# Attention over 4096 positions: where k's tiles and v's rows lie in SBUF

## The chip, the cores and the metric

The kernel runs on one core of one Trainium2 chip. The metric is the device time in microseconds: the median of 3 runs. Before the change it is 2519.33 us (2519.18 to 2519.79). The profile is of one execution, with a span of 2516.5 us and a mean granted TensorE clock of 0.999 of full speed.

## The reference

For each of 4 images of 64 x 64 positions with 256 channels, three projections q, k (128 channels each) and v (256 channels) are formed, then attention without a scale, then a sum with the input:

```
q = x @ Wq + bq; k = x @ Wk + bk; v = x @ Wv + bv     # float32
pq = q.reshape(B, -1, N); pk = ...; pv = ...          # N = 64 * 64 = 4096, a plain reshape
energy = einsum('bcn,bcm->bnm', pq, pk)
attention = softmax(energy, axis=-1)
out = gamma * einsum('bcm,bnm->bcn', pv, attention) + x
```

All is float32, and the result has to be nearly so.

## The kernel before

**Two programs.** The function has a fast program (lines 199 to 529), which takes exponentials without subtracting a maximum, and a general one (line 531 on), which runs only if the sums of the exponentials leave a range. The fast one checks that range at its end: `guard` (line 412) compares all sums `zall` with two limits, puts the answers in the tile `ok`, and reduces them to one word, `again`. In the profiled execution only the fast program ran.

**Splitting.** TensorE multiplies in float32r. To get nearly float32 from it, each operand is split into forms: h (an upper part, a slightly scaled rounded copy), l (what h leaves) and d (a combination of both). `halved` does this for q and k, `project_v` for v (vh, vl, vd), `upper` and `halves` for the exponentials. Each product then takes three matrix products: h with h, l with l, d with d.

**Tiling.** Per image, NG = 16 groups g of NB = 256 columns of output, and for each group NU = 8 steps t of 4 blocks of 128 positions: `STEPS` = 128 per image, 512 in all. One step does:

- `energy` (line 298): 12 products of 256 columns. The stationary operand (weights) is a 128 x 128 slice of the tile `k`, the moving one a form of the tile `q` (two runs of 128 columns). Results go to `sa` and `sb` in PSUM, and ScalarE takes exponentials into `x` and `y` (line 315).
- `join` (x times y, VectorE), `upper` (h, ScalarE), `halves` (l and d, VectorE).
- `attend` (line 344), twice: 12 products each, four with h and `vh`, four with l and `vl`, four with d and `vd`. The weights are slices of h, l or d; the moving operand is row m of v's form, with m = 2t, 2t + 16, 2t + 1, 2t + 17 for the four. The rows of `vh` and `vl` have C + 2 = 258 columns: 256 of v, and two of ones, which give the sums of the exponentials. Rows of `vd` have 256.

**Order.** The order of every engine's instructions is written out by hand (`manual_schedule`): the loop at line 490 puts step u's attention after the energies of step u + 3 (`LOOK`), so that TensorE always has work that does not wait for the exponentials. `load_k` (line 292) fetches k's forms from DRAM, 768 KB a step, five steps ahead into 3 buffers.

**Addresses.** A tile pool's tiles lie one after the other in SBUF, in the order const, xpool, xtpool, qkv, ppool, work, kpool; each buffer's size is rounded up to 32 bytes per partition. `q` (3072 bytes, 2 buffers), `r` and `ra` are in `work`, the tile `k` (6144 bytes, 3 buffers) and `f` (3072 bytes, 2 buffers) in `kpool`, which comes last. `vh` and `vl` are in `qkv`, `ok` and `zall` in `const`. The pools fill SBUF up to 128 bytes: the last buffer of k ends at byte 229,248 of 229,376.

The last group of the last image is finished by `finish_last` (line 427), all others by `whole` and `finish`; both take the factors `r` (gamma over the sums) from `factors` (line 377).

Of the kernel before, what the change touches and what calls it, by code (L numbers as in the profile page):

```python
# [9 lines left out]
F32 = mybir.dt.float32  # L10
F32R = mybir.dt.float32r
I32 = mybir.dt.int32
AF = mybir.ActivationFunctionType
ALU = mybir.AluOpType
# [6 lines left out]
def kernel(  # L21
# [36 lines left out]
    nc = tc.nc  # L58
    B, W, H, C = x.shape
    P = 128  # L60
    N = W * H
    C2 = C // 2
    NM = N // P
# [14 lines left out]
    const = ctx.enter_context(tc.tile_pool(name="const", bufs=1))  # L78
# [8 lines left out]
    ones = const.tile([P, P], F32, name="ones")  # L87
# [12 lines left out]
    gam = const.tile([P, 1], F32, name="gam")  # L100
# [73 lines left out]
    NB = 256  # L174
    NJ = NB // P
    NG = N // NB
    NU = NM // 4
    STEPS = NG * NU
    LOOK = 3
    E = 2.0**-12  # L180


# [1 line left out]

    again = const.tile([P, 1], I32, name="again")
    zs = const.tile([P, 1], F32, name="zs")
    ok = const.tile([P, B * NG * NJ], F32, name="ok")

    zall = const.tile([P, B * NG, NJ], F32, name="zall")
    bv4_sb = const.tile([P, KC], F32, name="bv4_sb")  # L190
    nc.gpsimd.tensor_scalar(bv4_sb, bv_sb, 1.0 / E, None, ALU.mult)

# [6 lines left out]
    with ExitStack() as fast:  # L199
# [4 lines left out]
        xpool, xtpool, qkv = pool("xpool", 3), pool("xtpool", 3), pool("qkv", 1)  # L204
        ppool, work, kpool = pool("ppool", 2), pool("work", 2), pool("kpool", 3)
# [3 lines left out]
        ps_t = pool("ps_t", 1, space=PSUM)  # L209


        vh = qkv.tile([P, NM, C + 2], F32R, tag="vh", name="vh")
        vl = qkv.tile([P, NM, C + 2], F32R, tag="vl", name="vl")
        vd = qkv.tile([P, NM, C], F32R, tag="vd", name="vd")
        for t in (vh, vl):
            nc.scalar.copy(t[:, :, C:], ones[:, : 2 * NM].rearrange("p (m t) -> p m t", t=2))

        images, qd, kf, units, loads, now = [], {}, {}, {}, {}, {}

# [13 lines left out]
        def image(b):  # L233
# [7 lines left out]
            def v_out(i):  # L241
                now["v4"] = work.tile([P, KC, C], F32, tag="v4", name=f"v4_{b}_{i}")
                return now["v4"], bv4_sb, 1.0 / E

# [7 lines left out]
        def halved(f, x):  # L252

            h = f[:, :, 0, :]
            nc.scalar.activation(h, x, AF.Identity, scale=UPPER / 64)
            for j, s, op in ((1, -64.0, ALU.add), (2, 64.0 * (1.0 + E), ALU.subtract)):
                nc.vector.scalar_tensor_tensor(
# [12 lines left out]
        def project_v(b, i):  # L270
# [3 lines left out]
            h = vh[:, m, :C]  # L274
            nc.scalar.activation(h, v4, AF.Identity, scale=UPPER * E)

            for t, f in ((vl, 1.0 / E), (vd, 1.0 / E + 1.0)):
                nc.vector.scalar_tensor_tensor(
# [19 lines left out]
        def energy(b, u, k):  # L298
# [10 lines left out]
            for i in range(2):  # L309
                for to, f, first, last in ((sa, 0, True, False), (sa, 1, False, True), (sb, 2, True, True)):  # L310
                    nc.tensor.matmul(  # L311
                        to[:, i], kt[:, 2 * k + i, f, :], q[:, :, f, :], start=first, stop=last
                    )
            for to, sp, scale in ((x, sa, (1.0 + E) / E), (y, sb, -1.0 / E)):
                nc.scalar.activation(  # L315
# [28 lines left out]
        def attend(b, u, j):  # L344
            g, t = divmod(u, NU)
            if t == j == 0:
                now["acc"] = [
                    ps_o.tile([P, C + 2], F32, tag=f"a{j}", name=f"a{j}_{b}_{g}")
                    for j in range(NJ)
                ]  # L350
                now["bb"] = ps_o.tile([P, NJ, C], F32, tag="bb", name=f"bb_{b}_{g}")
            h, l, d = units[b, u]
            a, bb = now["acc"][j], now["bb"]
            n = slice(j * P, (j + 1) * P)
            for out_, left, right in ((a, h, vh), (a, l, vl), (bb[:, j, :], d, vd)):
                for i in range(4):
                    m = 2 * t + i // 2 + NI * (i % 2)

                    nc.tensor.matmul(  # L359
                        out_,  # L360
                        left[:, i, n],
                        right[:, m, :],
                        start=(t == i == 0 and (left is h or left is d and j == 0)),
                        stop=(t == NU - 1 and i == 3 and left is not h),
                        skip_group_check=True,
                    )
            if t == NU - 1 and j == NJ - 1 and (b, g) != (B - 1, NG - 1):
                now["o"] = work.tile([P, NJ, C], F32, tag="o", name=f"o_{b}_{g}")
                nc.scalar.copy(now["o"], bb)

        def sums(b, g):
            for j in range(NJ):
                a = now["acc"][j]
                nc.vector.tensor_copy(zall[:, b * NG + g, j : j + 1], a[:, C : C + 1])

        def factors(b, g):

            r = work.tile([P, NJ], F32, tag="r", name=f"r_{b}_{g}")
            nc.vector.reciprocal(r, zall[:, b * NG + g, :])
            nc.vector.tensor_tensor(r, r, gam.to_broadcast([P, NJ]), ALU.mult)  # L380
            return r

        def whole(b, g):

# [7 lines left out]

        def finish(b, g, o, xr):
            yield
            r = factors(b, g)
            for j in range(NJ):
                nc.scalar.activation(  # L397
                    o[:, j, :], o[:, j, :], AF.Identity, scale=r[:, j : j + 1]
                )
            yield  # L400
            yield
            tp = ps_t.tile([P, 2, NB], F32, tag="t", name=f"ot_{b}_{g}")
            for s in range(2):
                for j in range(NJ):
                    nc.tensor.transpose(
                        tp[:, s, j * P : (j + 1) * P], o[:, j, s * P : (s + 1) * P], ident
                    )
            yield
            nc.vector.tensor_tensor(xr, xr, tp, ALU.add)
            nc.gpsimd.dma_start(ov[b, g], xr)  # L410

        def guard():

            z = zall.rearrange("p n j -> p (n j)")
            nc.vector.tensor_scalar(ok, z, Z_LOW, None, ALU.is_ge)
            nc.vector.scalar_tensor_tensor(ok, z, Z_HIGH, ok, ALU.is_le, ALU.mult)
            yield
            nc.vector.tensor_reduce(zs, ok, AX.X, ALU.min)
            nc.vector.tensor_scalar(zs, zs, 0.5, None, ALU.is_lt)
            zp = ps_s.tile([P, 1], F32, tag="b", name="zp")  # L420
            nc.tensor.matmul(zp, ones, zs, start=True, stop=True)
            yield
            nc.vector.tensor_copy(again, zp)
            yield
            yield

        def finish_last(b, g, xr):

            sums(b, g)
            r = factors(b, g)  # L430
            check = guard()
            ra = work.tile([P, NJ], F32, tag="ra", name="ra", bufs=1)
            nc.vector.tensor_scalar(ra, r, 1.0 + E, None, ALU.mult)
            o = work.tile([P, NJ, C], F32, tag="o", name=f"o_{b}_{g}")
            tps = []
            for j in range(NJ):
                next(check)
                nc.scalar.activation(
                    o[:, j, :], now["bb"][:, j, :], AF.Identity, scale=r[:, j : j + 1]
                )  # L440
                nc.vector.scalar_tensor_tensor(
                    o[:, j, :], now["acc"][j][:, :C], ra[:, j : j + 1], o[:, j, :], ALU.mult, ALU.add
                )
                tp = (ps_t, ps_s)[j].tile([P, 2, P], F32, tag="ta"[j], name=f"ot_{b}_{g}_{j}")
                for s in range(2):
                    nc.tensor.transpose(tp[:, s, :], o[:, j, s * P : (s + 1) * P], ident)
                tps.append(tp)
            for j in range(NJ):
                next(check)
                n = slice(j * P, (j + 1) * P)  # L450
                nc.vector.tensor_tensor(xr[:, :, n], xr[:, :, n], tps[j], ALU.add)
            nc.sync.dma_start(ov[b, g], xr)
# [18 lines left out]
        for b in range(B):  # L471
# [18 lines left out]
            for u in range(STEPS):  # L490
                g, t = divmod(u, NU)
                ahead = u + LOOK
                if ahead // NU + 1 < NG and ahead % NU == 3:
# [23 lines left out]
                for j in range(NJ):  # L517
                    attend(b, u, j)
                if (b, u) == (B - 1, STEPS - 1):
                    finish_last(b, g, loads.pop((b, "x", g)))  # L520
                elif t == NU - 1:
                    whole(b, g)
                    start(finish(b, g, now["o"], loads.pop((b, "x", g))))
# [7 lines left out]
    NB = 512  # L531
    NG = N // NB
    NJ = NB // P
    NP = NM // 2
    xg, og = columns(x, NB), columns(out, NB)
    with tc.If(nc.values_load(again[0:1, 0:1]) > 0), ExitStack() as general:
# [3 lines left out]
        xpool, xtpool, qkv = pool("gx", 2), pool("gxt", 2), pool("gqkv", 1)  # L540
        ppool, work = pool("gp", NP + 2), pool("gw", 1)
# [3 lines left out]
        for b in range(B):  # L545
# [16 lines left out]
            for g in range(NG):  # L562
                ps = []
                mx = work.tile([P, 2, NB], F32, tag="mx", name=f"gmx_{b}_{g}")
                for t in range(NP):
# [9 lines left out]
                    p = ppool.tile([P, 2, NB], F32, tag="p", name=f"gp_{b}_{g}_{t}")  # L575
# [52 lines left out]
                r = work.tile([P, NB], F32, tag="r", name=f"gr_{b}_{g}")  # L628
                nc.vector.reciprocal(r, zb)
                for s in range(2):  # L630
                    y = work.tile([P, NB], F32, tag="y", name=f"gy_{b}_{g}_{s}")
# [33 lines left out]
```

## Time and profile before

| | value |
|---|---|
| time, median of 3 | 2519.33 us |
| span of the profiled execution | 2516.5 us |
| LDWEIGHTS in `attend`, h / l / d | 189 ns each, 4096 of each kind |
| LDWEIGHTS in `energy` | 188 ns, 6144 |
| VectorE, join / l / d | 1222 / 1218 / 1218 ns, 512 of each |
| ScalarE, exponentials of sa / sb | 595 / 599 ns, 1024 of each |
| k's load | 512 of 768 KB, 4.8 us from issue to landing |
| DMA | 198 GB/s in the mean |

PE is TensorE's matrix products, PEld its loads of weights, which overlap the products; DVE is VectorE, ACT is ScalarE, POOL is GpSimd. In a group's row the figures after the bar are busy time in us and mean duration in ns, and after a second bar the idle time of the engine just before these instructions and what ended it. Products are pipelined: one starts long before the one ahead of it is at its end, so TensorE's pace has to be read from starts.

### The profile page before, as it was taken

What the parts mean: (1) busy time and instruction counts of PE and PEld (TensorE: products, weight loads), DVE (VectorE), ACT (ScalarE), POOL (GpSimd) and SP (SyncE); (2) the same over time, 40 slices, a digit from 0 to 9 for tenths busy, and PEclk for the clock granted to TensorE, in tenths of its full rate; (3) what the DMA queues carried; (4) which work ended last, traced back from release to release, by engine and by line L of the source; (5) the groups of instructions that cost most, each with busy time, mean ns of one, the idle gap of its engine ahead of it and who ended that gap; (6) DMA issues with size and microseconds to landing.
All of it is one profiled execution on the core that took longest, in us unless ns stands there. A gap on an engine that the chain in (4) does not pass through costs nothing.

```text
span 2516.5 us, 50017 instructions
## 1 busy us (share of the span) xinstructions
PE 2497.4 (99%) x19982; PEld 2455.1 (98%) x19982; DVE 2102.5 (84%) x2440; ACT 1806.1 (72%) x3138; POOL 424.6 (17%) x780
## 2 busy tenths in 40 slices
PE   9999999999999999999999999999999999999998
PEld 8999999999899999999989999999998999999998
DVE  5888888888688888888868888888886888888887
ACT  5777777776677777777667777777766777777775
POOL 4211111111411111111041111111114111111110
PEclk9999999999999999999999999999999999999999
DMA  7666666664766666666476666666648666666663
GB/s 238 214 192 210 198 203 197 193 207 147 236 214 189 206 198 201 201 191 205 138 243 220 194 192 207 200 206 194 190 143 254 213 197 195 201 200 206 198 191 108
DMA packets 137407, 498.92 MB, mean 198 GB/s; under 512 B 15536, under 2 KB 57264, under 8 KB 137168
## 3 DMA queue, kind: packets, MB, share of 16 engines
q0 software_dynamic: 92320, 453.17, 57.4%
q1 hardware_dynamic: 44304, 42.22, 5.6%
q8 instruction: 160, 2.62, 0.4%
q14 instruction: 79, 0.65, 0.1%
q10 hardware_dynamic: 544, 0.26, 0.0%
HBM read 445.25 MB, written 50.33 MB: 197 GB/s over the span
## 4 chain that ended last, share of the span: by engine, by line


## 5 line engine op out<-in xcount | busy, mean ns | idle before, releaser
L315 ACT ACTIVATE x<-sa 128x512 f32<-128x512 f32 x1024 | 609.5, 595 | 429.6 <-PE sa L311 367.6
L325 DVE TENSOR_TENSOR x<-x,y 128x1024 f32<-128x1024 f32 x512 | 625.4, 1222 | 172.9 <-ACT y L315 172.9
L311 PE MATMUL sa<-q,k 128*128 128x256 f32 x4096 | 759.2, 282 | 6.3 <-ACT x L315 6.0
L359 PE MATMUL a<-vh,h 128*128 128x258 f32 x4096 | 662.4, 284 | 0.0
L359 PE MATMUL a<-vl,l 128*128 128x258 f32 x4096 | 660.3, 283 | 0.0
L359 PE MATMUL bb<-vd,d 128*128 128x256 f32 x4096 | 651.9, 281 | 0.0
L311 PEld LDWEIGHTS sa<-q,k 128*128 128x128 f32 x4096 | 627.1, 188 | 8.0 <-ACT x L315 6.9
L336 DVE TENSOR_TENSOR l<-x,h 128x1024 fp32r<-128x1024 f32 x512 | 623.6, 1218 | 0.0
L339 DVE SCALAR_TENSOR_TENSOR d<-h,x 128x1024 fp32r<-128x1024 f32 x512 | 623.5, 1218 | 0.0
L315 ACT ACTIVATE y<-sb 128x512 f32<-128x512 f32 x1024 | 613.1, 599 | 0.0
L311 PE MATMUL sb<-q,k 128*128 128x256 f32 x2048 | 580.4, 283 | 0.0
L330 ACT ACTIVATE h<-x 128x1024 fp32r<-128x1024 f32 x512 | 543.5, 1061 | 34.9 <-DVE x L325 34.0
L359 PEld LDWEIGHTS a<-vl,l 128*128 128x128 f32 x4096 | 563.8, 189 | 0.0
L359 PEld LDWEIGHTS a<-vh,h 128*128 128x128 f32 x4096 | 561.5, 189 | 0.0
L359 PEld LDWEIGHTS bb<-vd,d 128*128 128x128 f32 x4096 | 557.6, 189 | 0.0
L295 POOL DMA_DIRECT2D k<-kf x512 | 279.7, 546 | 1508.1 <-PE sb L311 1476.0
L311 PEld LDWEIGHTS sb<-q,k 128*128 128x128 f32 x2048 | 385.4, 188 | 8.7 <-ACT y L315 0.8
L136 PE MATMUL qk<-wqk_sb,xts 128*128 128x256 f32 x512 | 121.5, 380 | 0.0
L157 PE MATMUL v<-xts,wv_sb 128*128 128x256 f32 x512 | 120.3, 379 | 0.0
L157 PEld LDWEIGHTS v<-xts,wv_sb 128*128 128x128 f32 x512 | 97.3, 190 | 13.2
L397 ACT ACTIVATE o<-o,r 128x256 f32<-128x256 f32 x126 | 57.4, 502 | 72.4 <-DVE r L380 72.4
L136 PEld LDWEIGHTS qk<-wqk_sb,xts 128*128 128x128 f32 x512 | 92.7, 191 | 10.1
(54 smaller groups left out, 884.5 us busy)
## 6 DMA issues: line engine op xcount, KB each, us to landing
k<-kf POOLq DMA_DIRECT2D x512, 768.0 KB, 4.8
x<-in_x_dram SPq DMA_DIRECT2D x128, 256.0 KB, 3.6
kf<-f POOLq DMA_DIRECT2D x64, 384.0 KB, 4.2
out_dram<-x POOLq DMA_DIRECT2D x63, 256.0 KB, 2.5
qd<-qks POOLq DMA_DIRECT2D x128, 64.0 KB, 2.9
qr<-qd SPq DMA_DIRECT2D x64, 128.0 KB, 3.1
wv_sb<-in_L_conv_Wv_dram POOLq DMA_DIRECT2D x1, 256.0 KB, 5.4
out_dram<-x SPq DMA_DIRECT2D x1, 256.0 KB, 3.9
```

What stands on the lines that cost most here:

```text
L136: nc.tensor.matmul(qk[:, s, :], self.xt[i][:, k, s, :], wqk_sb[:, k, :], start=(k == 0), stop=(k == KC - 1),)
L157: nc.tensor.matmul(vp[:, eh, :], wv_sb[:, k, eh * P : (eh + 1) * P], self.xt[i][:, k].rearrange("p s a -> p (s a)"), start=(k == 0), stop= ...
L295: nc.gpsimd.dma_start(t.rearrange("p (i s) f d -> p i s (f d)", s=2), kf[b, u % NU])
L311: nc.tensor.matmul(to[:, i], kt[:, 2 * k + i, f, :], q[:, :, f, :], start=first, stop=last)
L315: nc.scalar.activation(to[:, 2 * k : 2 * k + 2, :], sp.rearrange("p i j d -> p i (j d)"), AF.Exp, scale=scale,)
L325: nc.vector.tensor_tensor(x, x, y, ALU.mult)
L330: nc.scalar.activation(h, units[b, u], AF.Identity, scale=UPPER)
L336: nc.vector.tensor_tensor(l, x, h.bitcast(F32), ALU.subtract)
L339: nc.vector.scalar_tensor_tensor(d, h.bitcast(F32), 1.0 + E, x, ALU.mult, ALU.subtract)
L359: nc.tensor.matmul(out_, left[:, i, n], right[:, m, :], start=(t == i == 0 and (left is h or left is d and j == 0)), stop=(t == NU - 1 and ...
L397: nc.scalar.activation(o[:, j, :], o[:, j, :], AF.Identity, scale=r[:, j : j + 1])
```

## The change

It moves data in SBUF and leaves every arithmetic instruction as it was. Three things are done together:

- The rows of `vh` and `vl` become C + 4 = 260 floats apart instead of 258. The two columns of ones stay, and two more columns are never read: `attend` cuts the moving operand to the width of its output.
- `ok` is no longer a tile of its own; the range check at the end uses a buffer of `y`. That frees the 512 bytes that the longer rows take.
- `ra` is no longer a tile of its own but the second half of `r`.

What follows for the addresses is the aim: k's tiles come to lie 64 bytes, modulo 128, from q's, where they were 32 apart, and each row of vh and vl starts at a multiple of 16 bytes from the first.

```diff
+    VC = C + 4
...
-    ok = const.tile([P, B * NG * NJ], F32, name="ok")
...
-        vh = qkv.tile([P, NM, C + 2], F32R, tag="vh", name="vh")
-        vl = qkv.tile([P, NM, C + 2], F32R, tag="vl", name="vl")
+        vh = qkv.tile([P, NM, VC], F32R, tag="vh", name="vh")
+        vl = qkv.tile([P, NM, VC], F32R, tag="vl", name="vl")
...
-            nc.scalar.copy(t[:, :, C:], ones[:, : 2 * NM].rearrange("p (m t) -> p m t", t=2))
+            nc.scalar.copy(t[:, :, C : C + 2], ones[:, : 2 * NM].rearrange("p (m t) -> p m t", t=2))
...
-                        right[:, m, :],
+                        right[:, m, : out_.shape[1]],
...
-            r = work.tile([P, NJ], F32, tag="r", name=f"r_{b}_{g}")
-            nc.vector.reciprocal(r, zall[:, b * NG + g, :])
-            nc.vector.tensor_tensor(r, r, gam.to_broadcast([P, NJ]), ALU.mult)
-            return r
+            r = work.tile([P, 2, NJ], F32, tag="r", name=f"r_{b}_{g}")
+            nc.vector.reciprocal(r[:, 0, :], zall[:, b * NG + g, :])
+            nc.vector.tensor_tensor(r[:, 0, :], r[:, 0, :], gam.to_broadcast([P, NJ]), ALU.mult)
+            return r[:, 0, :], r[:, 1, :]
...
+            ok = ppool.tile([P, 4, NB], F32, tag="y", name="ok")[:, 0, : B * NG * NJ]
...
-            r = factors(b, g)
+            r, ra = factors(b, g)
             check = guard()
-            ra = work.tile([P, NJ], F32, tag="ra", name="ra", bufs=1)
```

More of the change, by code (lines that the diff above doesn't have):

```diff
@@ L394, in finish @@
             yield
-            r = factors(b, g)
+            r, _ = factors(b, g)
             for j in range(NJ):
@@ L429, in finish_last @@
             sums(b, g)
-            r = factors(b, g)
+            r, ra = factors(b, g)
             check = guard()
-            ra = work.tile([P, NJ], F32, tag="ra", name="ra", bufs=1)
             nc.vector.tensor_scalar(ra, r, 1.0 + E, None, ALU.mult)
```

## Prediction

> **What bounds the kernel now.** I read the page's busy times first, then the groups, then the waits, then the order of TensorE's work in one stretch.
>
> ```profile
> PE 2497.4 (99%) x19982; PEld 2455.1 (98%) x19982; DVE 2102.5 (84%) x2440; ACT 1806.1 (72%) x3138; POOL 424.6 (17%) x780
> ...
> L311 PE MATMUL sa<-q,k 128*128 128x256 f32 x4096 | 759.2, 282 | 6.3 <-ACT x L315 6.0
> L359 PE MATMUL a<-vh,h 128*128 128x258 f32 x4096 | 662.4, 284 | 0.0
> L359 PE MATMUL a<-vl,l 128*128 128x258 f32 x4096 | 660.3, 283 | 0.0
> L359 PE MATMUL bb<-vd,d 128*128 128x256 f32 x4096 | 651.9, 281 | 0.0
> ```
>
> TensorE has no idle time worth the name (6.3 us before the energies), so the span is the sum of its products' distances. The mean duration (282 ns) is not that distance, because products overlap. The chain of waits is empty for this trace. Among the waits the long ones are POOL's for a free buffer of k (1476 us, "POOL k L295 <- PE sb L311") and ACT's for scores: other engines waiting for TensorE. The distance comes from the order in time (start, length, count in a row):
>
> ```profile
> 302.76 0.40 PE L311 MATMUL sa<-q,k 128*128 128x256 f32 x2
> 303.00 0.28 PE L311 MATMUL sb<-q,k 128*128 128x256 f32 x1
> ...
> 304.17 0.64 PE L359 MATMUL a<-vh,h 128*128 128x258 f32 x4
> 304.64 0.64 PE L359 MATMUL a<-vl,l 128*128 128x258 f32 x4
> 305.12 0.64 PE L359 MATMUL bb<-vd,d 128*128 128x256 f32 x4
> ...
> 308.46 0.65 PE L359 MATMUL a<-vh,h 128*128 128x258 f32 x4
> ```
>
> One step (12 energies, 24 products with v) takes 308.46 - 304.17 = 4.29 us; the 12 energies before it 304.17 - 302.76 = 1.41 us, or 117.5 ns each. There are 512 steps, so 512 x 4.29 = 2196 us of 2516.5. The weights of the next product are fetched while the present one streams:
>
> ```profile
> 303.23 0.19 PEld L311 LDWEIGHTS sb<-q,k 128*128 128x128 f32 x1
> 303.35 0.31 PEld L311 LDWEIGHTS sa<-q,k 128*128 128x128 f32 x2
> ```
>
> The first load for the sa product of 303.46 starts at 303.35, as the sb product starts. Both operands are read from SBUF together, and the change alters only where they lie.
>
> **What the skill says.** "TensorE: Matmul & The Clock Gate", section "Wait — 56ns, not 53.3ns?", gives N / 2.4 + 2.5 ns between warm products: 109.2 ns for 256 columns, an estimate from that page. The trace has 117.5 at a granted clock of 0.999, so some 8 ns of each product are unexplained. The float32 projections, which pass twice as long, show no such loss: eight qk products from 665.84 to 667.57 us are 216 ns each, 512 / 2.4 + 2.5. "SBUF — State Buffer", section "Who interferes with whom", says that TensorE waits for nobody and gives it separate read ports for weights and moving data. The trace agrees for other engines: at one place of the group the distance repeats to under 1 ns, whenever the other engines start. It does not agree for the two TensorE reads, as the next part shows. The same page's specifications have 16-byte lines, with a penalty for crossing to a new one. No page has a rule on distances modulo 128.
>
> **Evidence on addresses.** I took the starts of neighbouring products from the trace and ordered them by the place t in the 8 steps of a group. A step at t uses v rows 2t, 2t+16, 2t+1, 2t+17. A row of vh or vl is 1032 bytes, so the row starts 8 bytes later, modulo 128, with each m; the weights (h, l) always start at 32, like vh and vl. So the distance of moving rows from weights is 8m modulo 128. The pace differs with t and hardly at one t: from h to h a step takes 4285 ns at t = 3, 4292 at t = 4 and 4303 at t = 5 in the median of 64 groups, and the 24 products of t = 3 spread by 0.5 ns (standard deviation), though VectorE's first instruction in that step starts anywhere from 0.25 to 0.30 us after it. So what changes with t is not the moment of other engines' work but the rows, or the products that went before. Mean distance of the 258-column products by that offset (t = 0, after a group's end, left out):
>
> - aligned to 16: 119.9 ns at 16, 119.8 at 32, 119.5 at 48, **118.6 at 64**, 119.5 at 80, 120.3 at 96, 121.7 at 112; mean 119.9
> - 8 past: 120.5, 119.5, 121.3, 121.5, 122.5, 120.9, 121.3 at 24 to 120; mean 121.1
>
> The weight load's own duration falls into two groups, 187 to 189 and 191 to 193 ns; the longer kind is 14% of loads at 64, 54% at 32, 56% at 96. So 64 is the quiet distance. q and k today are 32 apart (q's first buffer at byte 194,336, k's at 210,816, whose remainders by 128 are 32 and 0), and vd and d are 0 apart.
>
> **The change part by part.** *Layout.* Removing ok takes 512 bytes ahead of all pools; vh and vl grow by 2 x 32 x 4 = 256 each. Everything from ppool on stays where it was, q's remainder 32 included. r's two buffers stay in their rounded 32 bytes; ra's 32 go. So kpool moves down by 32 and k has remainder 96, 64 from q.
>
> *Energies.* 512 x 12 = 6144 products go from distance 32 to 64. The row for 258 columns has 119.8 against 118.6, so 1.2 ns less: 6144 x 1.2 = 7.4 us, all on the path, since TensorE never idles. The distance 64 was never seen for 256-column products, so I bound it: at best the page's floor of 109.2 against the measured mean of 117.8 (52.8 us less), at worst the slow pattern that bb shows at t = 5, 119.7 ns (11.7 us more).
>
> *Rows of v.* 512 x 16 = 8192 products. Half of them, those of odd m, go from 8-past to 16-aligned distances: 121.1 - 119.9 = 1.2 ns on 4096, 4.9 us. The lower bound is 0: bb, whose rows are all 1024 bytes apart, also takes 1.6 ns longer in the last two products of a group than in the first two, and odd m are always the last two. So the place, not the address, may be the reason. The upper bound is 2 ns on all 8192, 16 us: the present 120.9 against bb's 118.4 is 2.5 ns, of which two more columns explain 0.8.
>
> *Other engines.* VectorE and ScalarE write rows 1040 instead of 1032 bytes apart; their writes are 64 instructions of each kind at about 690 and 631 ns, hidden behind projections. Cost 0, hidden by TensorE. VectorE is busy 3.48 to 4.29 us of a 4.29 us step in five steps after a group's end, 86% on average, so a step shorter by 0.03 us is still covered.
>
> *DMA.* k's and f's tiles no longer start at a multiple of 128. k's load lands 4.8 us after issue. Between the last energy that reads a k buffer and the first of the tile three steps later lie 3 x 4.29 - 1.41 = 11.5 us; issue (0.55) and landing leave 6.1. Even a landing half as long again (7.2) is hidden. Cost 0.
>
> *Guard and factors.* ok is now a y buffer; its use comes after all joins on the same engine, so it adds no wait that is not over. ra becomes a slice of r: the same instruction (168 ns), once. Cost 0.
>
> Sum: -7.4 - 4.9 = -12.3 us; 2519.3 - 12.3 = **2507 us**.
>
> **Rivals.**
> - *Quiet distance in full*: at 64 the two reads never meet and energies run at the floor: -52.8 - 4.9, **2462 us**. For it: the loss of 8 ns per product is there to be had, and float32 products don't have it. Against it: the v products at distance 64 still take 118.6 ns for 258 columns, floor 110.
> - *Slow pattern*: the distance is not a property of one product but of a run of them. Energies with the same addresses repeat 117, 120, 117, 115, 118 ns at most t, but 122, 120, 116, 117, 119 ahead of t = 5. A new distance could settle into a slower run, such as bb's 119.7 at t = 5: +11.7, rows of v 0, **2531 us**, slower.
> - *Nothing*: place in the group explains v, and energies average out over the pattern. bb at distance 0 (118.4) and energies at 32 (117.8) differ by 0.6 ns only. **2519 us**.
>
> **How the numbers follow.** The forecast 0.50, quiet distance in full 0.12, slow pattern 0.24, nothing 0.14. The forecast's own spread (v alone or energies alone, 4.9 to 24 us less) leaves 0.02 of it within 0.2%. Faster: 0.48 + 0.12 = 0.60; same: 0.02 + 0.14 = 0.16; slower 0.24. The range goes down to 2475, where energies would stand at about 113 ns (the shortest distance seen repeatedly in bb, -29 us) and v at its upper bound (-16 us). It goes up to 2540, where energies would take the worst aligned v distance, 121.7 less 0.8 for two columns: 120.9 - 117.8 = 3.1 ns, 19 us. What is left out is most of the quiet distance and a tail of the slow pattern, some 0.18.
>
> **What would show it.** Right: 12 energies in 1.39 to 1.40 us instead of 1.41; pairs of places t and t + 4 alike in their v products, since 1040 bytes move the row by 16 and 8 rows by 128; groups of a<-vh and a<-vl at about 0.479 us instead of 0.483; TensorE still without idle time; k's landing under 7 us. Wrong: energies at 1.31 us (the first rival), or above 1.44 (the second); a wait of sa for k's transfer, or of the products for VectorE's l and d, would mean that something beside addresses set the time.

## The result, and the profile after

The changed kernel takes 2509.11 us (median of 4; 2508.76 to 2510.49) against 2519.26 us before: a ratio of 0.996, 95% interval 0.9943 to 0.9978, or 10.2 us less. From the profile's page after:

```profile
PE 2487.4 (99%) x19982; PEld 2446.0 (98%) x19982; DVE 2103.4 (84%) x2440; ACT 1804.9 (72%) x3138; POOL 424.4 (17%) x780
...
L311 PE MATMUL sa<-q,k 128*128 128x256 f32 x4096 | 749.9, 281 | 6.5 <-ACT x L315 6.3
L359 PE MATMUL a<-vh,h 128*128 128x258 f32 x4096 | 662.8, 284 | 0.0
L359 PE MATMUL a<-vl,l 128*128 128x258 f32 x4096 | 658.5, 283 | 0.0
L359 PE MATMUL bb<-vd,d 128*128 128x256 f32 x4096 | 655.6, 282 | 0.0
```

TensorE is still busy all the time, its idle time ahead of the energies is the same (6.5 for 6.3 us), and the other engines' rows have not moved. The 10 us are in the products themselves: sa's busy time is 9 us less, vl's 2 us less, and bb's 4 us *more*. The order of TensorE's work shows how (start, length, count). First the energies ahead of the step at t = 4, then those ahead of t = 5, each with the first h product that follows:

```profile
302.47 0.40 PE L311 MATMUL sa<-q,k 128*128 128x256 f32 x2
302.70 0.28 PE L311 MATMUL sb<-q,k 128*128 128x256 f32 x1
...
303.88 0.64 PE L359 MATMUL a<-vh,h 128*128 128x258 f32 x4
...
306.77 0.39 PE L311 MATMUL sa<-q,k 128*128 128x256 f32 x2
307.00 0.28 PE L311 MATMUL sb<-q,k 128*128 128x256 f32 x1
307.11 0.39 PE L311 MATMUL sa<-q,k 128*128 128x256 f32 x2
...
308.13 0.65 PE L359 MATMUL a<-vh,h 128*128 128x258 f32 x4
```

Twelve energies with the same distance of 64 take 1.41 us in one step and 1.36 us in the next. That is not a spread: from the starts in the trace, with each place t of a group taken by itself over the whole run, the twelve take 1413 to 1416 ns ahead of t = 2, 3 and 4 and 1361 ns ahead of t = 5, 6 and 7, with a standard deviation under 1 ns. In the slow case the distances repeat 118, 118, 117 ns; in the fast one they are 113, 113, 113. Before, they were 1408 to 1422 ns at all these places. So the changed kernel has **two patterns** at distance 64, and nothing between them at these six places. (The energies ahead of t = 0 and t = 1 follow the work at a group's end and are left out here and below.)

The next table adds up, for each kind of product, the time from its start to the next start on TensorE (us, waits included).

| | before | after | k alone | rows alone |
|---|---|---|---|---|
| energies, sa and sb | 752.7 | 742.1 | 737.9 | 755.0 |
| h with vh | 496.6 | 496.8 | 499.9 | 493.8 |
| l with vl | 493.8 | 491.8 | 492.9 | 492.7 |
| d with vd | 486.7 | 490.2 | 484.7 | 487.4 |

Not all of the column "after" comes from addresses and order. In the changed kernel's trace the granted clock falls to half in two stretches of 3.4 us, from 81.4 and from 1948.5 us on. In them 32 products with v take 94 ns more than elsewhere, 3.0 us together. The traces of the other three columns have no such stretch before the last 9 us of the run. Without these 3.0 us, the products with h, l and d took 495.8, 490.7 and 489.2 us. Why the clock fell there is not shown.

### The profile page after: what moved, and what is told of

Same layout as the page of the kernel before. It is cut to its first block, busy times and chain, and to the rows that moved or that the text cites. A ratio compares the mean times of both kernels' runs of the same rounds, so it can differ in the third digit from the quotient of the medians.

```text
span 2506.9 us, 50017 instructions
## 1 busy us (share of the span) xinstructions
PE 2487.4 (99%) x19982; PEld 2446.0 (98%) x19982; DVE 2103.4 (84%) x2440; ACT 1804.9 (72%) x3138; POOL 424.4 (17%) x780
## 4 chain that ended last, share of the span: by engine, by line
## 5 line engine op out<-in xcount | busy, mean ns | idle before, releaser
L311 PE MATMUL sa<-q,k 128*128 128x256 f32 x4096 | 749.9, 281 | 6.5 <-ACT x L315 6.3
```

The lines of the kernel that those rows point to most:

```text
L311: nc.tensor.matmul(to[:, i], kt[:, 2 * k + i, f, :], q[:, :, f, :], start=first, stop=last)
```

## The experiments

**Two halves of the change.** The first kernel moves k alone: `ra` becomes a part of `r`, the rows stay 258 floats, and `ok` keeps its tile. k's first buffer is then at byte 210,784 (remainder 96 by 128), q's at 194,336 (32), as in the changed kernel.

```diff
+            r = work.tile([P, 2, NJ], F32, tag="r", name=f"r_{b}_{g}")
...
-            ra = work.tile([P, NJ], F32, tag="ra", name="ra", bufs=1)
```

> Only k's tiles move: 64 bytes from q's modulo 128, rows of vh and vl stay 258 floats, the range check keeps its tile. Theory 1 (k's distance from q makes the gain): about 10 us faster than before, 2509 us, with energies at about 113 ns in some places of the group. Theory 2 (the rows of v, or what they leave behind for the energies, make it): within 3 us of before, 2519. Theory 3 (each half gives some of it): 4 to 6 us faster.

Measured: 2504.48 us, ratio 0.9946 (0.9933 to 0.996). The second has the rows and the range check of the changed kernel, and a pad that puts k back:

```diff
+        kpool.tile([P, 8], F32, tag="pad", name="pad", bufs=1)
```

> Only the rows of vh and vl are 260 floats apart (and the range check is in y); a pad of 32 bytes puts k back to where it was, 32 from q modulo 128. Theory 1: within 3 us of before, 2519 us, energies at 117 to 118 ns everywhere. Theory 2: about 10 us faster, 2509. Theory 3: 4 to 6 us faster, 2514.

Measured: 2521.01 us, ratio 1.0004 (0.9995 to 1.0012). From the groups of these two, first k alone, then rows alone:

```profile
L311 PE MATMUL sa<-q,k 128*128 128x256 f32 x4096 | 744.8, 280 | 6.4 <-ACT x L315 6.4
...
L311 PE MATMUL sb<-q,k 128*128 128x256 f32 x2048 | 576.4, 281 | 0.0
```

```profile
L313 PE MATMUL sa<-q,k 128*128 128x256 f32 x4096 | 761.2, 283 | 6.4 <-ACT x L317 6.0 <-DVE q L259 0.4
...
L313 PE MATMUL sb<-q,k 128*128 128x256 f32 x2048 | 580.6, 284 | 0.0
```

Moving k alone brings the whole gain; rows at multiples of 16 bytes bring none to the total. With k alone the energies are fast ahead of t = 4 to 7 (1361 to 1365 ns) and slow ahead of 2 and 3 (1416): one fast place more than in the changed kernel, which is worth 64 steps x 53 ns = 3.4 us. The two kernels' intervals overlap, so that k alone is the better one is likely from the traces (2.4 us in the table's sums without the half-clock stretches) and not shown by the times.

**Other distances.** The changed kernel with larger pads ahead of k:

```diff
+        kpool.tile([P, 16], F32, tag="pad", name="pad", bufs=1)   # 0 from q
+        kpool.tile([P, 24], F32, tag="pad", name="pad", bufs=1)   # 96 (q minus k)
```

> The changed kernel with k's tiles 0 from q's modulo 128 (a pad of 64 bytes ahead of k). If 64 is the one good distance: no energies at 113 ns, 2517 to 2525 us. If any distance other than 32 does: like the changed kernel, 2509. If distance 0 keeps the two reads in conflict all along: energies near 120 ns, 2525 to 2535.

> The changed kernel with k's tiles 32 bytes from q's on the other side, modulo 128 (q minus k is 96 instead of 64; before it was 32). If only 64 has a fast pattern: energies at 117 to 119 ns, 2515 to 2525 us. If the sign matters and 96 is a distance of its own: anything from 2500 to 2535.

Measured: 2519.97 us at distance 0, ratio 0.9998 (0.999 to 1.0007), and 2529.91 us at 96, ratio 1.0038 (1.0025 to 1.0051). The twelve energies at the places t = 2 to 7 take, by q minus k modulo 128:

| distance | twelve energies, ns | a run of distances |
|---|---|---|
| 0 | 1422 to 1430 | 122 120 119 115 117 |
| 32 (rows alone) | 1406 to 1427 | 117 120 117 115 118 among others |
| 64 (changed kernel) | 1361, or 1413 to 1416 | 113 113 113, or 118 118 117 |
| 96 | 1430 to 1438 | 125 116 123 118 121 117 |

At one place the standard deviation is at most 0.7 ns, so these differences are real. Distance 96 is slower than 32, so the sign counts: a wrong step of 32 bytes would have cost about 10 us (7.5 of it in the energies' sum, and some in two stretches at half the clock) where the right one brought 10. Of the four distances, 64 alone has a pattern with a mean under 117 ns.

**Does 64 help the d products too?** A pad of 64 bytes ahead of d:

```diff
+            if (b, u) == (0, 0):
+                ppool.tile([P, 16], F32, tag="pad", name="pad", bufs=1)
             d = ppool.tile([P, 4, NB], F32R, tag="d"
```

> The changed kernel with the tiles d 64 from vd's rows modulo 128 (a pad of 64 bytes ahead of d), k still 64 from q. If a distance of 64 is good for any pair of weights and moving rows: the bb products fall from 119.1 towards 113 to 115 ns, 4096 x 4 to 6 ns = 16 to 25 us, and the energies, which follow bb, run at 113.4 ns at all places of the group, 6144 x 2.7 = 16 us; 2465 to 2490 us. If it is special to the energies: within 5 us of the changed kernel, 2509. If runs of four are too short to settle: only the energies gain or lose by what state bb leaves behind, 2495 to 2520.

Measured: 2508.05 us, ratio 0.9953 (0.9938 to 0.9968). The products with d took 483.7 us instead of 490.2, at t = 4 with four in a row at 113 ns; but the energies after them fell into the slow pattern at five of six places (1412 to 1413 ns; 1380 at t = 5) and took 748.3 instead of 742.1 us. What one kind gained the next lost. Nothing of q or k had moved against each other, so what runs *before* the energies probably has a say in their pattern; the kernel with another order, below, tests that with no tile moved. This kernel also answers a rival. In all the others above, q stays and k alone moves, so k's own place could be what counts and not its distance from q. Here the pad moves q and k together: k has remainder 32, as in the kernel at distance 0, and yet the energies repeat 118, 118, 117 or 113, and not 122, 120, 119, 115, 117. So k's own place does not explain the pace; its distance from q does.

**The same order of addresses at all places.** If addresses and what runs before are all, making the places of a group equal in both must make their times equal. Rows of 288 floats (1152 bytes, 9 x 128) do that:

```diff
-    VC = C + 4
+    VC = 288
-    ... pool("xpool", 3) ...
+    ... pool("xpool", 2) ...                        # qks, v4, qr: bufs=1
+            if (b, u) == (0, 0):
+                ppool.tile([P, 16], F32, tag="pad", name="pad", bufs=1)
             h = ppool.tile([P, 4, NB], F32R, tag="h"
```

The pad ahead of h puts h, l and d 64 from their rows; the second kernel is without the pad, so that they stand 0 from them.

> Rows of vh and vl 288 floats (1152 bytes, a multiple of 128) apart, so that all v products have one distance, and h, l and d moved so that it is 64 for all of them, as it is for q and k. To make room, x, qks, v4 and qr have one buffer less each, which can cost some us in the projections. Theory A (each product has a pace by its own distance, 64 best): all products at 113 to 115 ns, 18,432 x 4 to 5 ns less than before, 2425 to 2450 us. Theory B (two patterns, a fast and a slow one, exist at distance 64, and what a change of operands leaves behind decides between them): energies either all fast (113.4 ns) or all slow (117.7), v products between 113 and 119; 2450 to 2520 us, places of the group nearly alike. Theory C (v products don't profit): 2505 to 2515.

> As the kernel with all distances 64 (rows of 1152 bytes, the same buffers cut), but h, l and d stand 0 from their v rows; q and k 64. It separates the distance of v's rows from their evenness and from the cut buffers. Theory A: v products near 119 to 120 ns, 2500 to 2515 us. Theory B: all places of the group alike, energies all fast or all slow: 2490 or 2515 us. If cut buffers cost: the projections at the start of each image are longer in the trace.

Measured: 2541.99 us, ratio 1.0083 (1.0066 to 1.01), with distance 64 everywhere; 2571.74 us, ratio 1.0205 (1.0188 to 1.0222), with v at 0. Both are slower; the steps are what matters here. Part of the loss lies between the images: from the first h product of an image's last step to that of the next image's first step pass 79 to 85 us with all distances 64, where it was 72, probably because of the cut buffers. Another part is the clock: 0.994 in the mean of that profile against 0.999, which is some 13 us by an estimate from these figures. From the order of TensorE's work with all distances 64, the first h product of the steps at t = 2, 3 and 4, and the energies between the last two:

```profile
305.53 0.64 PE L361 MATMUL a<-vh,h 128*128 128x258 f32 x4
...
309.75 0.64 PE L361 MATMUL a<-vh,h 128*128 128x258 f32 x4
...
312.61 0.40 PE L311 MATMUL sa<-q,k 128*128 128x256 f32 x2
...
312.96 0.39 PE L311 MATMUL sa<-q,k 128*128 128x256 f32 x2
...
313.98 0.64 PE L361 MATMUL a<-vh,h 128*128 128x258 f32 x4
```

All steps from t = 1 to t = 6 take 4227 ns (median of 64 each); before they took 4276 to 4303. Each repeats the same 36 distances, and the energies run 118, 117, 116, 114, then eight times 113: they start slow and fall into the fast pattern within four products. With v at distance 0 all steps from 2 to 6 take 4300 ns and the energies stay in the slow pattern (1416 ns in the median) at all six places, though q and k are 64 apart there as well; only ahead of t = 2 did 11 of the 64 groups run fast. This is the clearest reading of the case: the differences between places before the change came from the rows' addresses, and the pattern of the energies is decided by the products ahead of them. (The pad moves q and k together too, by 64 bytes; the next experiment moves nothing.) Yet the v products at a constant distance of 64 stayed at 118.5 to 119.4 ns: theory A, that each product's pace belongs to its own distance, falls.

**Another order, the same addresses.**

```diff
-            for out_, left, right in ((a, h, vh), (a, l, vl), (bb[:, j, :], d, vd)):
+            for out_, left, right in ((bb[:, j, :], d, vd), (a, h, vh), (a, l, vl)):
```

> As the kernel in which k's tiles alone moved, but each attend takes the products with d first, then h, then l, so that the energies follow an l product and not a d product. All addresses, counts and distances are the same. If distances alone set the energies' pace: the same energies, 115 ns in the mean, 2504 to 2509 us. If what ran before decides which of two patterns they fall into: other places of the group are fast, at 113.4 or 118.0 ns and nothing between; 2497 to 2516 us.

> The order d, h, l of the products in attend, as in the kernel with d first, but with all tiles where they are before the change (q and k 32 apart). It tells how much of the 21 us of that kernel is the order (shorter waits at a group's start) and how much k's distance. If the distance gives its part there too: 2507 to 2513 us here, energies 117.5 to 118.5 ns. If the order alone did it: 2497 to 2501.

Measured: with k moved 2498.97 us, ratio 0.9914 (0.9897 to 0.993); with all tiles as before 2506.72 us, ratio 0.9947 (0.993 to 0.9963). With k moved the fast places are now t = 4 and 5 alone (1370 to 1372 ns, with three slower products at the start), the others are at 1410 to 1414, where k alone in the old order was fast at 4 to 7: the pattern moved with the order, as theory B had it. But the time fell for a second reason. At a group's end, ScalarE copies bb out of PSUM. These are the waits of VectorE for that copy, and of the copy for bb, before; then those of the copy with d first and k moved (us in total, times, longest):

```profile
DVE o L389 <- ACT o L369: 58.6, 63, 0.9
ACT o L369 <- PE bb L359: 58.1, 63, 5.2
```

```profile
ACT o L369 <- PE bb L359: 12.6, 3, 4.2
```

With d first, bb is done eight products earlier, so the copy (587 ns) hardly waits, and VectorE no longer waits for the copy at all. So VectorE adds a to o and forms r earlier, and ScalarE's scaling of o by r, which stands in its queue ahead of exponentials that free sa and sb, comes earlier too. Before the change, the energies that need sa and sb have gaps. The first line below is the transposes at the group's end, then come the energies after them, and the next step:

```profile
289.29 0.60 PE L405 MATMUL ot<-ident,o 128*128 128x128 f32 x4
...
290.43 0.39 PE L311 MATMUL sa<-q,k 128*128 128x256 f32 x2
290.76 0.38 PE L311 MATMUL sb<-q,k 128*128 128x256 f32 x1
290.98 0.40 PE L311 MATMUL sa<-q,k 128*128 128x256 f32 x2
...
291.33 0.64 PE L359 MATMUL a<-vh,h 128*128 128x258 f32 x4
```

The same place with d first and k moved:

```profile
288.33 0.60 PE L405 MATMUL ot<-ident,o 128*128 128x128 f32 x4
...
289.46 0.39 PE L311 MATMUL sa<-q,k 128*128 128x256 f32 x2
289.69 0.28 PE L311 MATMUL sb<-q,k 128*128 128x256 f32 x1
289.81 0.39 PE L311 MATMUL sa<-q,k 128*128 128x256 f32 x2
...
290.14 0.64 PE L359 MATMUL bb<-vd,d 128*128 128x256 f32 x4
```

From 290.43 to 290.76 and on to 290.98 lie 0.33 and 0.22 us where d first has 0.23 and 0.12. These are waits of 0.1 us, which the profile's rows count as no idle time at all; the step at t = 0, from its first product with v to that of t = 1, takes 4939 ns before and 4698 with d first (4728 with all tiles as before). The two changes don't add up in full: 0.9947 x 0.9946 = 0.9894, measured 0.9914, probably because with d first two of the six places are fast and not four. **d first with k moved alone is the fastest version here**, 10 us under the changed kernel. Some 4 us of that are the clock, by an estimate from the mean clock of their executions (0.999 in all four, against 0.997 to 0.998).

**One column of k as the weights.** To see whether the two reads meet at all, the weight load of an energy reads a single place. It leaves out all of k but one column of each block, so it does not compute the attention:

```diff
-                        to[:, i], kt[:, 2 * k + i, f, :], q[:, :, f, :], start=first, stop=last
+                        to[:, i], kt[:, 2 * k + i, f, 0:1].to_broadcast([P, P]), q[:, :, f, :], start=first, stop=last
```

> As the kernel in which k's tiles alone moved, but the weights of each energy product are one column of k read 128 times (step 0), so that the weight load touches a single place in SBUF; what is computed is not the reference's. If the lost time of a product comes from the weights' read meeting the moving read: energies near 109 to 111 ns at all places. If it comes from the moving read alone or from the load as such: 113 to 118 ns as before, in two patterns. The v products, which are as they were, give the comparison: 118 to 121 ns.

Measured: 2505.56 us, ratio 0.9942 (0.9923 to 0.9962). From the order of its work, the energies ahead of t = 4:

```profile
304.26 0.39 PE L311 MATMUL sa<-q,k 128*128 128x256 f32 x2
304.49 0.28 PE L311 MATMUL sb<-q,k 128*128 128x256 f32 x1
...
305.63 0.64 PE L359 MATMUL a<-vh,h 128*128 128x258 f32 x4
```

1.37 us, 114 ns per product; ahead of t = 5 they take 1401 ns, in runs of 116, 117, 118; ahead of the other four places 1360 to 1369 ns. So the expected 109 to 111 ns did not come, and a slow case remains with weights that never leave one place. But t = 2 and 3, slow with k alone (1416), are fast here (1363), so how the weights are read probably bears on which pattern runs. Either a read of one place is fetched 128 times and meets the moving read there too, or the meeting is not what costs the time. The runs don't tell these apart.

**The even rows without cut buffers.** qks, v4 and o take turns in three buffers, and qr lies in a buffer of f's; once with the old order of attend, once with d first.

```diff
-... tag="qk", name=f"qks_{b}_{i}")
+... tag="o", name=f"qks_{b}_{i}", bufs=3)           # v4 and o likewise
+            t = kpool.tile([P, 2, 3, P], F32, tag="f", name=f"qr_{b}_{g}", bufs=2)[:, :, 0, :]
```

> The kernel with all distances 64 and rows of 1152 bytes, without the cut buffers: qks, v4 and o take turns in three buffers, qr lies in f's. Seven places of a group at 4227 ns as there, against 4285 in the mean before: 512 x 0.058 x 7/8 = 26 us less, and the projections as before: 2490 to 2498 us. If the shared buffers make waits in the projections: 2500 to 2540.

> The same with the order d, h, l in attend. If the shorter waits at a group's start (10 to 16 us) add to it, and the energies fall into the fast pattern at all places: 2470 to 2485 us. If they fall into the slow one after an l product: 12 x 512 x 3.5 ns = 21 us more, 2495 to 2505. All places of a group should be alike either way.

Measured: 2525.07 us, ratio 1.0021 (1.0014 to 1.0028), and 2522.55 us, 1.001 (1.0003 to 1.0016). My sum for the first was 27 to 35 us too low. The steps did what they should (4227 ns at t = 2 to 6); from the start of an image's first step of attention to that of its last lie 547 to 549 us where it was 553. But from there to the next image's first step it took 76 to 79 us instead of 72, and the first image's attention began at 82.2 instead of 75.0 us: three shared buffers are probably too few. With d first, the energies were slow at all six places (1413 ns), a case that its expectation named, though not at the 2495 to 2505 us given for it. Nor were all places alike: ahead of t = 1, where the energies follow the transposes and 201 ns pass from the first start to the second, the rest run 120, 117, 116, 114, then 113. The distance is one and the same at all places, so this too comes from what ran before.

## Why the prediction was right or wrong

**What bounds the kernel: right.** TensorE's distances are the span, no engine took its place, and k's load landed after 4.8 us as before.

**Layout: right.** k moved to a remainder of 96 and q stayed.

**Energies: right in sign and near in size, for the wrong reason.** Predicted 7.4 us less, measured 752.7 - 742.1 = 10.6. The prediction took 1.2 ns off each product. In truth the twelve energies ahead of t = 5, 6 and 7 take 48 to 61 ns less, 4 to 5 ns each, and those ahead of t = 2, 3 and 4 take 2 to 8 ns more. "Slow pattern", the rival, was half of what happened: a distance has patterns of its own, and which one runs is settled by what precedes. "Quiet distance in full" did not occur; the fast pattern is 113 ns, not 109.

**The table of distances, on which that step stood, was no property of the distances.** When k alone moved, the v rows and their weights kept every address, and yet the mean of 258-column products went from 118.6 to 119.9 ns at distance 64 and from 119.8 to 121.6 at 32. The products with v inherited another state from the energies ahead of them. I had named this ("or the products that went before") and then averaged over it. The table also leaves out the first product after the energies, which takes 130 ns at t = 3. And the weight loads don't single out 64: longer ones are 14% there, but 12% at 104, where products take 120.9 ns. That 64 came out best for the energies is shown by the runs; that I could have known it from that table is not.

**Rows of v: wrong.** Predicted 4.9 us less; the three kinds of v products together took 1477.1 us before and 1478.8 after, 1475.7 without the half-clock stretches, and the rows alone gave 1.0004. The step that failed is that each kind of product was priced with the others held still. The products with h and l did take 3.9 us less, in the changed kernel (without those stretches) and with rows alone. But the products with d, whose distance the change leaves alone, took 2.6 and 0.7 us more, and with rows alone the energies took 2.3 more. Nor can the 3.9 us be put down to even rows: with k alone, whose rows did not change, h and l took 2.4 us more. The bound of 0 was the right end for the total, but not for the reason that stood beside it: the last two products of a group of four (h and l, the one after the energies left out) take 1.3 ns more than the first two in the changed kernel and 0.1 ns more with rows alone, whose rows are the same.

**The sum: near by luck.** -7.4 - 4.9 = -12.3 against -10.2: the first term was 3 too small, the second nearly 7 too large, and 3.0 of these 7 are the clock, which the prediction held constant.

**The signs I named.** "Energies in 1.39 to 1.40 us" was not seen at any of the six places; it was 1.41 or 1.36. "Places t and t + 4 alike" failed for three of four pairs (the 24 v products, from the first start to the last: 2761 and 2770 ns at 1 and 5, 2747 and 2775 at 2 and 6), probably because equal addresses follow different energies; but it held for 3 and 7 (2733 both), which follow slow and fast ones too.

**Reads that disturb nobody.** The Trainium skill's page "SBUF — State Buffer", section "Who interferes with whom", gives TensorE two read ports of its own and lets it wait for nobody. The pace by distance (1361 to 1438 ns for the same twelve products) does not fit that as it stands, and the measurement decides; by what mechanism stays open. The page's specifications give 16-byte lines and a price for crossing to a new one; that rows start 8 bytes past such a line cost nothing that the time of a run here shows (1.0004).

**Open.** What the state is that passes from one product to the next. Also, five executions of the kernel with k alone lie in two heaps (2504.2 to 2504.5 and 2509.0 to 2509.6 us); a place that flips between patterns from run to run would give steps of 3.4 us. But the mean clock is 0.999 in the three faster ones and 0.998 and 0.997 in the two slower, and 0.001 of 2504 us is 2.5 us, so stretches at half clock, as in the changed kernel's trace, are the likelier reason. Only one of the five was profiled, a fast one without such a stretch before its end.

## What to carry to other kernels

When TensorE is busy throughout, read the distance of starts, not durations, and compare one kind of product at each place of the loop: if it is constant to a nanosecond at a place and differs between places, operand addresses and the order of products may be at work, as they were here. Take out stretches at a lower granted clock before comparing sums of two traces: here they were 3 us of a change of 10. Move one operand by 32 bytes at a time and measure each; do not sum single-product averages, because a product's pace depends on those before it. Look also at waits of 0.1 us that no idle column shows: moving one group of products within a step was worth as much as the addresses.

## What the runs showed of the hardware that was not expected

- Float32r products of 256 columns ran at 113 to 120 ns on average, by the operands' distance modulo 128 and by what ran before, in repeating runs of one to six products (113; 118 118 117; 117 120 117 115 118). In the changed kernel twelve of them at one place of a group had a standard deviation of at most 0.7 ns over the whole run.
- With equal addresses at all places, steps of 36 products mostly repeat to the nanosecond (medians of 4227 or 4300 ns), while DMA, VectorE and ScalarE run beside them.
- The same twelve products with the same distance of 64 have two stable paces, 113.4 and 118 ns, 4% apart.
- A weight load that reads one column 128 times did not make the product faster than 113 ns.
- With a mean granted clock of 0.998, the loss was not spread over the run: it lay in two stretches of 3.4 us at half clock and one at the end, and each product with v inside the first two took 94 ns more.
